# First sums of q's and k's inner products by ScalarE, and the place of three small steps, in an attention and non-local block

## The chip, the cores and the metric

The kernel runs on one core of a Trainium2 chip. The metric is the device time of one execution in microseconds; the value given for a kernel is the median of several runs. All tensors are float32.

## What is computed

The input x has 8 images of 512 channels and 32 x 32 positions. Two layers follow each other:

```
# layer 0, 8 heads of 64 channels
q, k, v = conv1x1(x, Wq, bq), conv1x1(x, Wk, bk), conv1x1(x, Wv, bv)
attn = softmax(q^T k / 8)                     # per image and head, 1024 x 1024
x = x + conv1x1(attn applied to v, Wp, bp)
# layer 1, 256 inner channels, n = 1024
g, theta, phi = conv1x1(x, ...), conv1x1(x, ...), conv1x1(x, ...)
z = conv1x1((theta phi^T / n) g, W_w, W_b) + x
out = batch norm of z over images and positions, per channel
```

A 1x1 convolution is a matrix product over the channels.

## The kernel before, in words

**Products with seven blocks.** Each convolution is a 2 x 2 block product done with seven block products instead of eight (`seven`, lines 254 to 302). The blocks of the data are differences t1 to t4 of quarters of x (`more_sums`), those of the weights are kept in DRAM with their sums. The table `SEVEN` (line 220) has one entry per block product: its name, which weight block, which data block, which PSUM slot it accumulates in, and into which quarters ("11", "12", "21", "22") of the result the slot is read when the product is there. The first read of a quarter writes it, on ScalarE or VectorE with the bias (`first`); later ones add the slot to the quarter on VectorE (`add`). A quarter has 2 x 128 channels and 512 positions; a slot has two PSUM banks, one for each 128 channels (index m), of 512 positions.

**A second level.** In q and k of images 1 to 7 three of the seven block products are themselves done with seven smaller ones (`nested`, lines 236 to 252; products 1, 6 and 2 of the outer seven, for the quarters "11", "12" and "21"), and the other four are full ones (`FOUR`, line 232). A full product has four matmuls of 128 x 128 by 512, called units here: m = 0 with both halves of the contraction, then m = 1. So a stage has 16 units. An inner product is one matmul of 128 x 128 by 256, called a step; there are 21. An inner step's result is read at once into 256 columns of q or k: added on VectorE, or written by ScalarE (line 373) where it is the first into its place. Before the change only the third of the three nested products, for "21", writes first; the quarters "11", "22" and "12" are written by ScalarE from the full products (line 380), and the inner products for "11" and "12" are added behind. The inner products alternate between two slots of PSUM; where the next one goes to the place of the last but one, it waits for the read of that.

**The order.** `STEPS` (line 233) says after which unit how many inner steps are issued; TensorE's order is fixed as written (`pe`). `fills` are small pieces of VectorE work called after certain units: the differences t3 and t4, and those for the second level of t4 (`inner_parts`); in k, the differences of the attention's output o for the projection that follows. VectorE's operations that are wrapped in `dve` keep their written order among each other; the others are placed by the framework's planner, which works with estimated durations and takes first what comes first in the program and can run. In q all adds are wrapped, in k only the fills.

**The stages of an image b**: attention (64 iterations of scores, exponential and weighted sums), then q, v, k of image b + 1, the projection of b with Wp, theta and phi, then g, the small products f and wf, and z. VectorE finds the maximum of the absolute values of each row of q and of k (lines 384 to 394, four instructions each), from which a bound on the scores is worked out (`bound_scores`, with a small matmul between the theta/phi products). In theta/phi, the functions in `between` are called after the product of that number: the maxima of k, all four, after number 1, the bound after number 4.

**The value bias.** The bias bv of the values is carried through Wp into bp once, in image 0 before the projection (`join_bias`, lines 174 to 189): GpSimd multiplies and adds Wp's rows into a tile wp_bv, eight small matmul records sum it over the channels, and VectorE adds the result to bp. wp_bv is taken from a ring of ten tiles that most temporary blocks share (`block`, line 76). The pool `w3` has three tiles with the tag "acc", for the sums of the exponentials and for g.

Of the kernel before, what the change touches and what calls it, by code (L numbers as in the profile page):

```python
# [8 lines left out]
F32 = mybir.dt.float32  # L9
I32 = mybir.dt.int32  # L10
AF = mybir.ActivationFunctionType
ALU = mybir.AluOpType
# [4 lines left out]
P = 128  # L17
# [13 lines left out]
def unshifted(ctx: ExitStack, tc: tile.TileContext, a: dict, out: bass.AP):  # L31
# [37 lines left out]
    def bank(tag, name):  # L69
        return psum.tile([P, 2, 512], F32, tag=tag, name=name)  # L70
# [5 lines left out]
    def block(name):  # L76
        return ring.tile([P, 2, 512], F32, tag="e", name=name)
# [95 lines left out]

    def join_bias(w):

        t = block("wp_bv")
        half = C // 2
        for m, quarters in enumerate(((w[:, 0], w[:, 1]), (corner["WpT"], w[:, 2]))):
            to, one = (t[:, i, m * half:(m + 1) * half] for i in range(2))
            for c in range(CC):  # L180
                nc.gpsimd.tensor_scalar(one if c else to, quarters[c // 2][:, c % 2, :], bv[:, c:c + 1], 1.0,
                                        ALU.mult, ALU.mult)
                if c:
                    nc.gpsimd.tensor_tensor(to, to, one, ALU.add)
        ps = next_bank("pbp")[:, 0, :CC]
        for oc in range(CC):
            pe(nc.tensor.matmul(ps[:, oc:oc + 1], t[:, 0, oc * P:(oc + 1) * P], ones, start=True, stop=True,
                                skip_group_check=True))
        nc.vector.tensor_tensor(bp, bp, ps, ALU.add)
# [26 lines left out]
    def quarters_of(t):  # L216
# [12 lines left out]
    FIVE = (SEVEN[0], SEVEN[1], SEVEN[2], SEVEN[3], ("s3t3", 5, "t3", 0, (("22", False), ("21", False))))  # L229


    FOUR = (SEVEN[0], ("s1t1", 3, "t1", 1, (("12", True), ("22", True))), ("s2t2", 4, "t2", 0, (("12", False),)),
            FIVE[4])
    STEPS = {2: [0] * 4 + [1] * 14, 3: [0, 0, 0, 1, 1, 2, 2, 2, 2, 2, 2, 3, 1, 1, 1, 1]}

    def nested(name, stage, w, data, tags, first, add):

        slots = [bank(tag, f"{name}_in_{tag}") for tag in tags]
        goes_to = {1: ("11", "21", False), 6: ("12", "22", False), 2: ("21", "t4", True)}
        for n, (q, di, begins) in enumerate(goes_to[i] for i in INNER[stage]):  # L240
            a, d = inner_blocks(w, stage, n), data[f"inner {di}"]
            pair = slots[::-1] if n % 2 else slots
            begun = set()
            for _, wi, di, s, reads in SEVEN:
                ps = pair[s % 2 if s < 2 else 1][:, s // 2, n % 2 * 256:(n % 2 + 1) * 256]
                pe(nc.tensor.matmul(ps, a[wi], d[di], start=s not in begun, stop=True, skip_group_check=True))  # L246
                begun.add(s)
                for to, is_first in reads:
                    c = rows(q).start + int(to[0]) - 1
                    at = cols(q).start + (int(to[1]) - 1) * 256  # L250
                    (first if is_first and begins else add)((slice(c, c + 1), slice(at, at + 256)), ps)
                yield

    def seven(name, w, data, positions_out, first, add, between=None, early=False,
              by_chunk=False, inner=None, fills=()):

        nk, half = w.shape[2], w.shape[3]
        tags = list(free)  # L260
        free[:] = [tags[3], tags[1], tags[0], tags[2]] if early else [tags[3], tags[1], tags[2], tags[0]]
        slots, begun = {}, set()
        steps, three = iter(()), inner and len(INNER[inner]) == 3
        unit, counts = 0, iter(STEPS[len(INNER[inner])] if inner else ())
        if inner:
            free[:] = [tags[1], tags[2], tags[3], tags[0]]
            steps = nested(name, inner, w, data, tags[2:], first, add)

        def read(reads, ps):
            for to, is_first in reads:  # L270
                (first if is_first else add)(to, ps)

        for n, (what, wi, di, s, reads) in enumerate(FOUR if three else FIVE if inner else EARLY if early else SEVEN):
            if s not in slots or early and what == "t4":
                slots[s] = bank(tags[s], f"{name}_{s}_{n}")
                begun -= {one for one in begun if one[0] == s}
            ps, d = slots[s], data[di]
            if positions_out:
                parts = [(ps.rearrange("p h (i f) -> p (h i) f", f=half)[:, i, :], i * half // 512,
                          lambda k, i=i: d[:, k, i * P:(i + 1) * P], lambda k: w[:, wi, k, :])  # L280
                         for i in range(512 // P)]
            else:
                parts = [(ps[:, m, :], m, lambda k, m=m: w[:, wi, k, m * P:(m + 1) * P], lambda k: d[:, k, :])
                         for m in range(half // P)]
            work = [(*part, k) for part in parts for k in range(nk)]
            if by_chunk and n == 0:
                work.sort(key=lambda one: one[4])
            for to_ps, at, lhsT, rhs, k in work:
                pe(nc.tensor.matmul(to_ps, lhsT(k), rhs(k), start=(s, at) not in begun, stop=(k == nk - 1),  # L289
                                    skip_group_check=True))  # L290
                begun.add((s, at))
                if three and unit in (3, 7, 11):
                    read(reads, ps)
                for _ in range(next(counts, 0)):
                    next(steps)
                if unit in fills:
                    fills[unit]()
                unit += 1
            if not three or n == 3:
                read(reads, ps)  # L300
            if between and n in between:
                between[n]()

# [61 lines left out]
    def heads_of(b, what, w, bias, data, pin=lambda ins: None, later=None, **how):  # L365

        t = mats.tile([P, CC, N], F32, tag=what, name=f"{what}_{b}")
        peak = small.tile([P, CC], F32, tag=f"peak_{what}", name=f"peak_{what}_{b}")

        def first(q, ps):  # L370
            if isinstance(q[0], slice):
                c = q[0].start
                nc.scalar.activation(t[:, c, q[1]], ps, AF.Identity, bias=bias[:, c:c + 1])
                return
            for m in range(2):
                c = rows(q).start + m
                if how.get("early") and q == "21":
                    nc.vector.tensor_scalar(t[:, c, cols(q)], ps[:, m, :], bias[:, c:c + 1], 1.0, ALU.add, ALU.mult)
                else:
                    nc.scalar.activation(t[:, c, cols(q)], ps[:, m, :], AF.Identity, bias=bias[:, c:c + 1])  # L380

        seven(f"p{what}_{b}", w, data, False, first, add_to(t, pin), **how)

        def peaks():
            for c in range(CC):
                ins = nc.vector.tensor_reduce(peak[:, c:c + 1], t[:, c, :], AX.X, ALU.max, apply_absolute_value=True)  # L386
                if b == 0 or later is not None:
                    dve(ins)

        if later is None:  # L390
            peaks()
        else:
            later.append(peaks)
        return t, peak

    def values(b, w, data, between=None):
# [398 lines left out]
    for b in range(B):  # L795
# [5 lines left out]
        def near_end():  # L801
            if not last:
                nxt["data"] = data_sums(quarters_of(nxt["x"]), f"x_{b + 1}", (1, 2))
                inner_sums(nxt["data"], "22")
            elif "data" not in nxt:
                nxt["data"] = data_sums(quarters_of(held["x"]), f"x1_{b - 1}_again", (1,))
            elif "t2" not in nxt["data"]:
# [9 lines left out]
        if not last:  # L817
            inner_sums(nxt["data"], "21", dve)
            later, of_t4 = [], []
            fills = {4: lambda: more_sums(nxt["data"], (3,), dve), 5: lambda: more_sums(nxt["data"], (4,), dve),  # L820
                     8: lambda: (of_t4.extend(inner_parts(nxt["data"], "t4", dve)), of_t4[0](), of_t4[1]()),
                     9: lambda: (of_t4[2](), of_t4[3]())}
            q, peak_q = heads_of(b + 1, "q", weights("WqT"), bq, nxt["data"], dve, inner="WqT",
                                 later=later, fills=fills)
            load_w(nc.sync)
# [1 line left out]
            def norm():  # L827
                nxt["products"] = normalize(denominators(next_bank(f"den_{b}")[:, 0, :]))

            v = values(b + 1, weights("WvT"), nxt["data"], {1: norm, 2: later[0], 5: lambda: nxt["products"]()})  # L830
            load_w(nc.sync)

            nxt["o"], of_21 = data_sums(quarters_of(o), f"o_{b}", ()), []
            fills = {unit: lambda i=i: more_sums(nxt["o"], (i,), dve) for unit, i in ((4, 1), (6, 2), (8, 3), (12, 4))}
            if b:
                fills[13] = lambda: (of_21.extend(inner_parts(nxt["o"], "21", dve)), of_21[0](), of_21[1]())
                fills[14] = lambda: (of_21[2](), of_21[3]())
# [30 lines left out]
        elif b > B - LATE and b != B - 2:  # L868
            z[b] = [xt[:, cc, :] for cc in range(CC)]
        tp = theta_phi(b, weights("tp"), data, {} if last else  # L870
                       {1: later_k[0], 4: lambda: bound_scores(b + 1, q, k, peak_q, peak_k)})
        load_w(nc.sync)

        def before_wf():
# [237 lines left out]
```

## Time and profile before

| | us |
|---|---|
| median of 5 runs | 2163.47 |
| lowest and highest run | 2161.86, 2164.29 |
| the profiled execution's own time | 2162.37 |
| its span, first to last instruction | 2160.5 |
| TensorE busy | 2131.9 |
| VectorE busy | 1401.3 |
| ScalarE busy | 744.8 |
| GpSimd busy | 202.0 |

The profile is of one execution. Times in it are counted from the span's start. PE is TensorE's matmul, PEld its weight load, which runs beside the matmul before; DVE is VectorE, ACT ScalarE, POOL GpSimd. An operation's line in the source is given as L and a number, and its tiles as out<-in by their names in the program: pq and pk are the PSUM slots of the full products of q and k, pq_in_s and pk_in_s those of the inner ones, ptp those of theta and phi, pbp that of the bias. One fp32 matmul of the program shows as two matmul records.

One image takes some 265 us from the start of one attention to the next; for image 2 the stages begin at 614.3 (attention), 724.3 (q of image 3), 747.5 (v), 773.1 (k), 796.3 (projection), 819.5 (theta and phi), 844.2 (g) and 866.6 (z). For image 0, k of image 1 begins at 237.8 and the projection at 264.0.

### The profile page before, as it was taken

The numbers are of one execution on the slowest core, as the hardware profiler recorded it, in microseconds if no ns is written. First come the engines' busy times: TensorE is split into PE (matmuls) and PEld (weight loads), VectorE is DVE, ScalarE is ACT, GpSimd is POOL, SyncE is SP. The second block draws the span as 40 slices with busy tenths as digits, with TensorE's granted clock in tenths as the row PEclk, the third lists the DMA queues.
The fourth block names the chain that finished last, engine by engine and source line by source line (L and its number), as shares of the span: only waits on it lengthen the run. The fifth ranks groups of instructions, "written<-read, shape, count | busy, mean of one in ns | idle before, by whom it ended". The sixth has DMA issues, their size and how long they took to land.

```text
span 2160.5 us, 30098 instructions
## 1 busy us (share of the span) xinstructions
PE 2131.9 (99%) x12510; PEld 1121.5 (52%) x12510; DVE 1401.3 (65%) x1690; ACT 744.8 (34%) x854; POOL 202.0 (9%) x256
## 2 busy tenths in 40 slices
PE   9999999999999999999999999999999999999996
PEld 4534664346733567335663366633666347643462
DVE  6467656676566675766657676576674676756736
ACT  1464103641046310463105621056212651056106
POOL 0111100110001100011000110011000110001000
PEclk9999999999999999999999999999999999999998
DMA  6333443334143331433324343233434235122758
GB/s 220 137 47 60 141 155 122 47 53 149 72 127 50 80 115 72 132 48 77 115 83 124 50 93 96 105 106 49 108 133 156 40 48 138 52 58 39 222 201 338
DMA packets 53375, 229.97 MB, mean 106 GB/s; under 512 B 9712, under 2 KB 16112, under 8 KB 45680
## 3 DMA queue, kind: packets, MB, share of 16 engines
q1 hardware_dynamic: 41552, 198.21, 27.2%
q0 software_dynamic: 10192, 28.46, 10.9%
q8 instruction: 100, 1.64, 0.3%
q10 hardware_dynamic: 1488, 1.32, 0.2%
q14 instruction: 43, 0.35, 0.0%
HBM read 140.79 MB, written 46.27 MB: 87 GB/s over the span
## 4 chain that ended last, share of the span: by engine, by line
PE 91%; DVE 5%; ACT 2%; DMA 1%; POOL 0%; issue 0%; ACTq 0%; POOLq 0%; SPq 0%
PE ps L450 20%; PE po L476 20%; PE pv L289 9%; PE pp L289 7%; PE pk L289 5%; PE pq L289 5%; PE ptp L289 5%; PE pg L289 4%; PE pq_in_s L246 3%; PE pk_in_s L246 3%; PE pf L616 3%; PE pz L289 2%; PE pp_in_s L246 2%; DVE peak_k L386 1%; PE pwf L651 1%; DVE tp L601 1%
## 5 line engine op out<-in xcount | busy, mean ns | idle before, releaser
L453 ACT ACTIVATE e<-ps 128x1024 f32<-128x1024 f32 x512 | 522.7, 1024 | 426.6 <-PE ps L450 421.1
L459 DVE TENSOR_TENSOR acc<-acc,e 128x1024 f32<-128x1024 f32 x384 | 470.0, 1224 | 144.3 <-ACT e L453 140.8
L476 PE MATMUL po<-e,v 64*64 64x512 f32 x4096 | 528.7, 589 | 0.7 <-ACT w_WgT L618 0.7
L450 PE MATMUL ps<-q,k 64*64 64x512 f32 x4096 | 529.1, 589 | 0.0
L476 PEld LDWEIGHTS po<-e,v 64*64 64x64 f32 x4096 | 156.5, 133 | 283.4 <-issue 275.7
L450 PEld LDWEIGHTS ps<-q,k 64*64 64x64 f32 x4096 | 155.6, 133 | 284.1 <-issue 275.0
L489 POOL DMA_DIRECT2D fold<-acc x189 | 147.1, 779 | 984.2 <-DMA fold<-acc 576.3
L457 DVE TENSOR_TENSOR acc<-e,e 128x1024 f32<-128x1024 f32 x64 | 78.3, 1224 | 144.0 <-ACT e L453 144.0
L639 ACT ACTIVATE g<-pg,gb 128x512 f32<-128x512 f32 x31 | 21.3, 687 | 379.6 <-PE pg L289 379.5
L289 PE MATMUL pv<-w_WvT,t_x 128*128 128x256 f32 x512 | 116.4, 381 | 0.0
L289 PE MATMUL ptp<-w_tp,t_x 128*128 128x256 f32 x512 | 115.2, 380 | 0.3
L289 PEld LDWEIGHTS pv<-w_WvT,t_x 128*128 128x128 f32 x512 | 96.6, 190 | 18.5 <-issue 5.7
L289 PEld LDWEIGHTS ptp<-w_tp,t_x 128*128 128x128 f32 x512 | 96.7, 190 | 16.0 <-DVE tp L601 3.1
L289 PE MATMUL pp<-t_o,w_WpT 128*128 128x512 f32 x208 | 100.8, 592 | 0.0
L289 PE MATMUL pq<-t_x,w_WqT 128*128 128x512 f32 x200 | 100.0, 593 | 0.8 <-DVE w_WqT L778 0.8
L289 PE MATMUL pk<-t_x,w_WkT 128*128 128x512 f32 x200 | 100.0, 592 | 0.0
L417 POOL TENSOR_SCALAR q<-q,gates 128x1024 f32<-128x1024 f32 x32 | 35.1, 1109 | 676.3 <-DVE gates L415 582.4
L405 ACT COPY v<-pv 128x1024 f32<-128x1024 f32 x32 | 32.4, 1012 | 173.2 <-PE pv L289 173.2
L289 PE MATMUL ptp<-w_tp,x 128*128 128x256 f32 x384 | 87.4, 381 | 0.0
L289 PE MATMUL pv<-w_WvT,x 128*128 128x256 f32 x384 | 86.8, 379 | 0.0
L289 PEld LDWEIGHTS ptp<-w_tp,x 128*128 128x128 f32 x384 | 72.4, 190 | 13.0 <-issue 3.6
L289 PEld LDWEIGHTS pv<-w_WvT,x 128*128 128x128 f32 x384 | 73.0, 190 | 10.3 <-issue 0.2
(179 smaller groups left out, 2255.3 us busy)
## 6 DMA issues: line engine op xcount, KB each, us to landing
fold<-acc POOLq DMA_DIRECT2D x189, 128.0 KB, 3.1
w_WqT<-kept_WqT SPq DMA_DIRECT2D x7, 2368.0 KB, 8.8
w_WkT<-kept_WkT SPq DMA_DIRECT2D x7, 2368.0 KB, 9.0
r<-den_d SPq DMA_DIRECT2D x32, 512.0 KB, 7.5
x<-in_x_dram SPq DMA_DIRECT2D x31, 512.0 KB, 5.9
w_WpT<-kept_WpT SPq DMA_DIRECT2D x6, 2176.0 KB, 8.5
w_WvT<-kept_WvT SPq DMA_DIRECT2D x7, 1792.0 KB, 7.1
w_tp<-kept_tp SPq DMA_DIRECT2D x7, 1792.0 KB, 7.2
```

Source lines behind the costliest of these rows:

```text
L246: pe(nc.tensor.matmul(ps, a[wi], d[di], start=s not in begun, stop=True, skip_group_check=True))
L289: pe(nc.tensor.matmul(to_ps, lhsT(k), rhs(k), start=(s, at) not in begun, stop=(k == nk - 1), skip_group_check=True))
L386: ins = nc.vector.tensor_reduce(peak[:, c:c + 1], t[:, c, :], AX.X, ALU.max, apply_absolute_value=True)
L405: seven(f"pv_{b}", w, data, True, lambda q, ps: nc.scalar.copy(at(q), as_v(ps)), lambda q, ps: dve(nc.vector.tensor_tensor(at(q), at(q), a ...
L417: nc.gpsimd.tensor_scalar(q[:, p, :], q[:, p, :], gate[:, p:p + 1], 1.0, ALU.mult, ALU.mult)
L450: pe(nc.tensor.matmul(ps[c * P // 2:(c + 1) * P // 2, j, :], k[r, p, keys], q[r, p, h * 512:(h + 1) * 512], start=True, stop=True, skip_gr ...
L453: nc.scalar.activation(e, ps, AF.Exp, scale=SCALE)
L457: nc.vector.tensor_tensor(accs[u], es[u, 0], e, ALU.add)
L459: ins = nc.vector.tensor_tensor(accs[u], accs[u], e, ALU.add)
L476: pe(nc.tensor.matmul(ps[j * D:(j + 1) * D, r, :], v[keys, m, (2 * p + j) * D:(2 * p + j + 1) * D], e[keys, j, :], start=(m == 0), stop=(m ...
L489: nc.gpsimd.dma_start(to, part_of, accum_op=ALU.add)
L616: pe(nc.tensor.matmul(ps[:, c, :], tp[:, i, c * P:(c + 1) * P], tp[:, i, CI:], start=(i == 0), stop=(i == NB - 1)))
```

## The change

- In q and k with three nested products, the first read of every place by an inner product is a write with the bias on ScalarE, for all three nested products. The full products of "11" and "12" are added behind by VectorE; the product "11" in slot 0 by halves (m = 0 after unit 6 and ahead of its steps, m = 1 behind them), the product into "12" in slot 0 by halves too (after units 9 and 11, ahead of the steps). "22" is still written first from slot 1 by ScalarE, now behind unit 9, and slot 1 is added to "12" by VectorE behind unit 11. The last product is added to "22" and "21" at the end, as before.
- `STEPS` for three nested products is arranged anew, with at most two steps behind a unit.
- The fills of q move from units 4, 5, 8, 9 to 3, 4, 5, 7; the first two of k from 4 and 6 to 3 and 5.
- The four maxima of k are called in pairs after theta/phi's products 1 and 2. Those of q are called together where they were.
- wp_bv is taken from the pool `w3` with the tag "acc", not from the ring.
- The four inner differences of "22" at the end of an attention keep their written order on VectorE.

```diff
     def join_bias(w):
-        t = block("wp_bv")
+        t = w3.tile([P, 2, 512], F32, tag="acc", name="wp_bv")
...
-    FOUR = (SEVEN[0], ("s1t1", 3, "t1", 1, (("12", True), ("22", True))), ("s2t2", 4, "t2", 0, (("12", False),)),
-            FIVE[4])
-    STEPS = {2: [0] * 4 + [1] * 14, 3: [0, 0, 0, 1, 1, 2, 2, 2, 2, 2, 2, 3, 1, 1, 1, 1]}
+    FOUR = tuple((*one[:4], ()) for one in (SEVEN[0], SEVEN[1], SEVEN[2], FIVE[4]))
+    AHEAD = {6: ((0, 0, "11", False),), 9: ((0, 0, "12", False),), 11: ((0, 1, "12", False),)}
+    BEHIND = {6: ((0, 1, "11", False),), 9: ((1, None, "22", True),), 11: ((1, None, "12", False),),
+              15: ((0, None, "22", False), (0, None, "21", False))}
+    STEPS = {2: [0] * 4 + [1] * 14, 3: [0, 0, 0, 1, 2, 2, 2, 2, 1, 2, 2, 2, 2, 1, 1, 1]}
...
-                    (first if is_first and begins else add)((slice(c, c + 1), slice(at, at + 256)), ps)
+                    (first if is_first and (begins or three) else add)((slice(c, c + 1), slice(at, at + 256)), ps)
...
+        def read_parts(parts):
+            for s, m, to, is_first in parts if three else ():
+                if m is None:
+                    read(((to, is_first),), slots[s])
+                else:
+                    c = rows(to).start + m
+                    read((((slice(c, c + 1), cols(to)), is_first),), slots[s][:, m, :])
...
-                if three and unit in (3, 7, 11):
-                    read(reads, ps)
+                read_parts(AHEAD.get(unit, ()))
                 for _ in range(next(counts, 0)):
                     next(steps)
+                read_parts(BEHIND.get(unit, ()))
                 if unit in fills:
                     fills[unit]()
                 unit += 1
-            if not three or n == 3:
-                read(reads, ps)
+            read(reads, ps)
...
-                inner_sums(nxt["data"], "22")
+                inner_sums(nxt["data"], "22", dve)
...
-            fills = {4: lambda: more_sums(nxt["data"], (3,), dve), 5: lambda: more_sums(nxt["data"], (4,), dve),
-                     8: lambda: (of_t4.extend(inner_parts(nxt["data"], "t4", dve)), of_t4[0](), of_t4[1]()),
-                     9: lambda: (of_t4[2](), of_t4[3]())}
+            fills = {3: lambda: more_sums(nxt["data"], (3,), dve), 4: lambda: more_sums(nxt["data"], (4,), dve),
+                     5: lambda: (of_t4.extend(inner_parts(nxt["data"], "t4", dve)), of_t4[0](), of_t4[1]()),
+                     7: lambda: (of_t4[2](), of_t4[3]())}
...
-            fills = {unit: lambda i=i: more_sums(nxt["o"], (i,), dve) for unit, i in ((4, 1), (6, 2), (8, 3), (12, 4))}
+            fills = {unit: lambda i=i: more_sums(nxt["o"], (i,), dve) for unit, i in ((3, 1), (5, 2), (8, 3), (12, 4))}
...
-                       {1: later_k[0], 4: lambda: bound_scores(b + 1, q, k, peak_q, peak_k)})
+                       {1: lambda: [one() for one in later_k[:2]], 2: lambda: [one() for one in later_k[2:]],
+                        4: lambda: bound_scores(b + 1, q, k, peak_q, peak_k)})
```

More of the change, by code (lines that the diff above doesn't have):

```diff
@@ L229, in unshifted @@
     FIVE = (SEVEN[0], SEVEN[1], SEVEN[2], SEVEN[3], ("s3t3", 5, "t3", 0, (("22", False), ("21", False))))
-    FOUR = (SEVEN[0], ("s1t1", 3, "t1", 1, (("12", True), ("22", True))), ("s2t2", 4, "t2", 0, (("12", False),)),
-            FIVE[4])
-    STEPS = {2: [0] * 4 + [1] * 14, 3: [0, 0, 0, 1, 1, 2, 2, 2, 2, 2, 2, 3, 1, 1, 1, 1]}
+    FOUR = tuple((*one[:4], ()) for one in (SEVEN[0], SEVEN[1], SEVEN[2], FIVE[4]))
[3 more added lines that the diff above has]
+    STEPS = {2: [0] * 4 + [1] * 14, 3: [0, 0, 0, 1, 2, 2, 2, 2, 1, 2, 2, 2, 2, 1, 1, 1]}
     def nested(name, stage, w, data, tags, first, add):
-        slots = [bank(tag, f"{name}_in_{tag}") for tag in tags]
+        slots, three = [bank(tag, f"{name}_in_{tag}") for tag in tags], len(INNER[stage]) == 3
         goes_to = {1: ("11", "21", False), 6: ("12", "22", False), 2: ("21", "t4", True)}
@@ L382, in heads_of, with peak_of @@
         seven(f"p{what}_{b}", w, data, False, first, add_to(t, pin), **how)
[L384 to L393, printed above, removed]
+        def peak_of(c):
+            ins = nc.vector.tensor_reduce(peak[:, c:c + 1], t[:, c, :], AX.X, ALU.max, apply_absolute_value=True)
+            if b == 0 or later is not None:
+                dve(ins)
+        for c in range(CC):
+            if later is None:
+                peak_of(c)
+            else:
+                later.append(lambda c=c: peak_of(c))
         return t, peak
@@ L828, in norm @@
                 nxt["products"] = normalize(denominators(next_bank(f"den_{b}")[:, 0, :]))
-            v = values(b + 1, weights("WvT"), nxt["data"], {1: norm, 2: later[0], 5: lambda: nxt["products"]()})
+            v = values(b + 1, weights("WvT"), nxt["data"], {1: norm, 2: lambda: [one() for one in later], 5: lambda: nxt["products"]()})
             load_w(nc.sync)
             nxt["o"], of_21 = data_sums(quarters_of(o), f"o_{b}", ()), []
-            fills = {unit: lambda i=i: more_sums(nxt["o"], (i,), dve) for unit, i in ((4, 1), (6, 2), (8, 3), (12, 4))}
+            fills = {unit: lambda i=i: more_sums(nxt["o"], (i,), dve) for unit, i in ((3, 1), (5, 2), (8, 3), (12, 4))}
             if b:
```

## The prediction

> **What bounds the kernel now.** I read the page's first part, then the chain of work that ended last, then the waits, and then TensorE's timeline inside one image.
>
> ```profile
> PE 2131.9 (99%) x12510; PEld 1121.5 (52%) x12510; DVE 1401.3 (65%) x1690; ACT 744.8 (34%) x854; POOL 202.0 (9%) x256
> ...
> PE 91%; DVE 5%; ACT 2%; DMA 1%; POOL 0%; issue 0%; ACTq 0%; POOLq 0%; SPq 0%
> ```
>
> TensorE (PE) is busy for 2131.9 of 2160.5 us, and the change removes no matmul. So it can win only stretches in which TensorE stands still or runs slowly, and it loses by making new ones. Work given from VectorE (DVE, 65%) to ScalarE (ACT, 34%) is worth nothing by itself. The stretches inside an image are short; the waits name them:
>
> ```profile
> POOL wp_bv L181 <- PE pk L289: 45.6, 1, 45.6
> ...
> PEld pq_in_s L246 <- ACT q L373: 3.7, 7, 0.5
> PEld pk_in_s L246 <- ACT k L373: 3.7, 7, 0.5
> PEld ptp L289 <- DVE tp L601: 3.1, 7, 0.4
> ...
> PEld pbp L187 <- POOL wp_bv L184: 2.2, 2, 1.4
> ```
>
> The columns are: who waited, for whom, us in total, times, longest. Seven times each (once per image) a weight load waits for ScalarE in q and in k, and for VectorE in theta/phi; once the bias waits for GpSimd (POOL). How much of such a wait TensorE itself feels, its timeline shows (start, duration; a group of two records is one fp32 matmul):
>
> ```profile
> 739.83 1.02 PE L289 MATMUL pq<-t_x,w_WqT 128*128 128x512 f32 x2
> 740.69 0.59 PE L246 MATMUL pq_in_s<-t_x,w_WqT 128*128 128x256 f32 x2
> 741.12 1.43 PE L246 MATMUL pq_in_s<-i_t_x,w_WqT 128*128 128x256 f32 x4
> 742.38 1.02 PE L289 MATMUL pq<-t_x,w_WqT 128*128 128x512 f32 x2
> ```
>
> From start to start a full matmul (a unit) takes 0.86 us and an inner one (a step) 0.43. The two steps from 741.12 should end at 741.98; the next unit starts at 742.38. That is a **stall of 0.40 to 0.41**: three steps stand in a row, and the third writes the bank whose first product ScalarE reads only from 741.32:
>
> ```profile
> 741.32 0.91 ACT L373 ACTIVATE q<-pq_in_s,bq 128x256 f32<-128x256 f32 x2 [4.90 <-PE pq_in_s L246]
> ```
>
> The product ends at 741.12, the read begins 0.20 later and takes 0.47, and TensorE goes on some 0.16 after it: a bank is blocked for 0.83 us from the end of its product, and one step covers 0.43. I counted the rest of q and of k against 0.86 and 0.43: apart from 0.1 to 0.2 at q's start nothing else is lost. The group of 1.43 stands in all fourteen stages.
>
> [...] The stall of 0.40 is a write held back by a read of the very same columns, so this trace does not tell bank from address; I take the bank, the stricter of the two. [...] The trace shows one such window in the body, right after image 0's k:
>
> ```profile
> 261.91:265.33 3.42, 2.38 (x11) 1.65 (x12) 2.13 (x4) 0.00 (x0) 1.51 (x3) 1.00 0.76 228
> 265.33:268.74 3.41, 3.41 (x5) 1.33 (x4) 0.69 (x1) 0.00 (x0) 0.00 (x0) 0.50 0.02 5
> ```
>
> The column before the last two is the granted clock: 0.50 for 3.41 us, following a window in which TensorE mostly waited for the bias. [...] Here, beside GpSimd's bias work, a difference t_o took 1.51 us instead of 1.22 and a GpSimd sum up to 1.71 instead of 0.72[...].
>
> **Part by part.** *Inner products in q and k.* Removed: the stall, for the new table of steps has at most two in a row: 14 x 0.41 = 5.7 us. Moved: of 21 inner reads per stage ScalarE now does 12 (4 before), VectorE 9 (17); ScalarE writes 2 full halves (0.6 each) where it wrote 6; VectorE gets 4 half adds (0.61 apart) for "11" and "12", and keeps three whole ones. VectorE: 8 x 0.34 less, 4 x 0.61 more, about 0.3 less; ScalarE: 8 x 0.45 more, 4 x 0.6 less, 1.2 more in a stage of 23 us with 70% idle. Both are beside TensorE.
>
> Does a new wait come? I placed the new order with 0.86 and 0.43 from the stage's start. Between a bank's product and the next into it there is now at least a unit and a step, 1.29 us, against 0.83 needed: **0.46 to spare**, also where two products come together, as ScalarE's second read then ends 0.44 after the first. VectorE is free of the preceding attention 4.4 us into q (728.71 less 724.30). Then t3 and t4 (1.14 each) end at 6.7, the adds of steps 3 and 4 at 7.9 (ready at 7.1; needed at 8.4), the two differences at 8.6, and the first half of "11" at 9.2. Unit 8 overwrites that half at 10.75: **1.4 to spare**. The second half waits for step 6 on ScalarE (9.7) and ends at 10.4; behind it on VectorE are the last two differences, wanted at 16.8. Around unit 9 the half add of "12" and two inner adds end at 14.5, and step 13 wants the bank at 15.05: 0.4 to spare. In k the products of the normalisation end at 2.8, and t2_o stands ahead of "11": that half is read by 9.6, 1.0 to spare. The last two whole adds begin at the stage's end as before. ScalarE's pair for "22" may be queued late, as written, or early, when slot 1 is complete: 1.2 us in front of inner reads that have 0.46 to spare, of which much then has arrived anyway; from 0 to 0.4 per stage, and I take 0.
>
> *Earlier differences* (fills), pinned order in the end of attention: 0 us; the trace already has that order, and their ring slots are released. The cover is VectorE's idle time; without it the 1.0 above shrinks.
>
> *Maxima of k in pairs.* Now four of 1.13 stand between two theta/phi sums:
>
> ```profile
> 829.69 3.62 PE L289 MATMUL ptp<-w_tp,x 128*128 128x256 f32 x16
> 833.36 3.72 PE L289 MATMUL ptp<-w_tp,t_x 128*128 128x256 f32 x16
> ```
>
> and on VectorE beside it:
>
> ```profile
> 827.58 4.59 DVE L386 TENSOR_REDUCE peak_k<-k 128x1 f32<-128x1024 f32 x4
> 832.09 1.21 DVE L601 TENSOR_TENSOR tp<-ptp,tpb 128x1024 f32<-128x1024 f32 x1
> ```
>
> Sixteen records take 3.455 elsewhere; here 3.67 pass: 0.21 lost, as slot 0 is read only at 832.1 to 833.2. After two maxima (to 829.85) that read runs 829.9 to 831.1, two us early; the other pair ends at 833.4 and the bound's matmul wants it at 836.9. Saved 7 x 0.21 = **1.5 us**; next late is nothing for 2 us.
>
> *Value bias.* wp_bv waited for a ring slot (45.6 above) until 254.6; its inputs were asked for from 237.9, landing in 3.0 to 6.4 us, so from about 244 it can run in another pool whose slot's last user is long done. Its 14 instructions took 8.9 us: done by about 254, and k's matmuls end at 261.1. TensorE then stood to 264.03, 2.91 us; the eight bias records themselves need some 1.04 (0.52 for four loads), so **1.9 us** goes. With it I let the half-clock window go: 3.41 x 0.5 = **1.7 us**; bounds 0 and 1.7, and the first is a rival. Against it, GpSimd now works beside k's weight sums on VectorE; eight or so such operations longer by up to 0.3 each, with 0.4 to spare: 0 to 0.6, I take 0.3.
>
> **Sum.** 5.7 + 1.5 + 1.9 + 1.7 - 0.3 = 10.5 us. The profiled execution took 2162.37 (span 2160.5) and would take 2151.9; the median of the runs is 1.1 higher, 2163.47, and gives **2153.0**. For this case alone 2150.5 to 2155.5: the unknown 0 to 0.6 and 0 to 1.7, and runs that lie 1.2 around their median.
>
> **Rivals.** (1) *The half-speed window stays*[...]: 1.7 less, 2154.7. [...] Against: idle time there falls from 2.9 to about 1. (2) *A wait takes the place of the one removed*: ScalarE's "22" pair or VectorE's half adds hold an inner bank 0.4 longer than its 0.46, in each stage. Then the 5.7 goes back: 2158.7, gain 4.8. For it: spares of 0.4 are thin; against: no other engine is near full there. (3) *Slower*: the first half of "11", until now read by ScalarE at unit 3, is behind VectorE's queue. If VectorE comes to it two long differences (2 x 1.14 = 2.3) later than I placed it, unit 8 stalls by 2.3 less 1.2 (mean of 1.4 and 1.0), 1.1 in each of 14 stages, and the later adds push on the next stage: 15.4 lost, with the rest 4.9 net, 2168.4. It costs from 1.0 to 1.4 us of lateness on, and outweighs all gains from about 2.0. For it: k's adds are not pinned, so the planner may put the pinned differences first; against: the trace of before keeps the written order in both stages.
>
> **How the numbers follow.** Forecast 0.56; rival 1 0.08; rival 2 0.23; rival 3 0.13. About 0.2%, 4.3 us, is what a measurement of this kernel can tell from no change. Rival 2 lies close to that edge: I put 0.10 of it faster, 0.13 within. Faster 0.56 + 0.08 + 0.10 = 0.74, same 0.13, slower 0.13. The range runs from the forecast's low end, 2150.5, past rival 2 with 2.3 on top, 2161.0, and leaves out mainly rival 3.
>
> **What would show it.** Right: no group of four inner records over 1.03 us in q and k; the two waits on ScalarE at L373 gone or without a gap on TensorE; q and k 0.4 shorter; 3.46 between the fourth and fifth theta/phi product; wp_bv's first instruction near 244 and no granted 0.50 near 265. Wrong: a wait of full matmuls (pq, pk at their line) for VectorE at the start of the third product, or of inner ones for ScalarE, seven times each, or wp_bv still starting after 254.

## The result and the profile after

The changed kernel takes 2166.45 us (median of 27 runs, 2165.44 to 2167.21). The kernel before, run beside it, takes 2162.0 (47 runs, 2160.06 to 2164.29). The ratio is 1.0021, with a 95% interval from 1.0016 to 1.0026: slower by 4.5 us, with the interval clear of no change. The forecast was 10.5 us faster. The profiled execution took 2166.16 us with a span of 2164.5, against 2162.37 and 2160.5 before.

The page's busy times and its chain of work that ended last:

```profile
PE 2133.9 (99%) x12510; PEld 1121.5 (52%) x12510; DVE 1395.4 (64%) x1634; ACT 761.3 (35%) x910; POOL 205.4 (9%) x256
...
PE 95%; ACT 2%; DVE 1%; DMA 1%; issue 0%; SPq 0%; DVEq 0%; ACTq 0%
```

TensorE has the same 12510 instructions, and the work did move: VectorE is 5.9 us lighter and ScalarE 16.5 heavier. TensorE's share of the chain even rose, from 91 to 95%, while the time grew. So neither of these views says where the time went. The waits do (who waited, for whom, us in total, times, longest):

```profile
POOL wp_bv L181 <- DMA w_WpT<-in_WpT_dram: 32.1, 1, 32.1
...
PEld pk_in_s L249 <- DVE k L323: 16.2, 28, 1.6
...
PEld pq_in_s L249 <- DVE q L323: 9.8, 28, 0.7
...
PEld pk_in_s L249 <- ACT k L383: 6.7, 28, 0.2
PEld pq_in_s L249 <- ACT q L383: 6.4, 27, 0.2
```

The seven long waits of a weight load for ScalarE (0.5 each) are gone from q and from k; short ones of at most 0.2 have come. But in k an inner product now waits up to 1.6 us for VectorE. TensorE's timeline in k of image 3 shows it (start, duration):

```profile
779.06 0.60 PE L249 MATMUL pk_in_s<-x,w_WkT 128*128 128x256 f32 x2
779.49 0.59 PE L249 MATMUL pk_in_s<-i_x,w_WkT 128*128 128x256 f32 x2
779.92 1.02 PE L300 MATMUL pk<-t_x,w_WkT 128*128 128x512 f32 x2
781.70 0.70 PE L249 MATMUL pk_in_s<-x,w_WkT 128*128 128x256 f32 x2 [0.76 <-DVE k L323]
782.24 0.60 PE L249 MATMUL pk_in_s<-i_x,w_WkT 128*128 128x256 f32 x2
...
785.25 0.60 PE L249 MATMUL pk_in_s<-i_x,w_WkT 128*128 128x256 f32 x2
785.83 1.13 PE L300 MATMUL pk<-t_x,w_WkT 128*128 128x512 f32 x2
786.79 0.60 PE L249 MATMUL pk_in_s<-x,w_WkT 128*128 128x256 f32 x2
```

I count units and steps from 0, as the tables in the code do. These lines are steps 5 and 6, unit 7, then steps 7 and 8. Unit 7 starts at 779.92, so step 7 is due at 780.78; it starts at 781.70, **0.92 late**, and step 8 comes 0.54 after it instead of 0.43, another 0.11. Further down unit 10 is due at 785.68 and starts at 785.83, and the step behind it comes after 0.96 instead of 0.86: 0.15 and 0.10. Unit 12 loses the same 0.25. VectorE's timeline beside it:

```profile
778.04 0.78 DVE L323 TENSOR_TENSOR k<-k,pk_in_s 128x256 f32<-128x256 f32 x2 [2.46 <-PE pk_in_s L249]
778.74 1.22 DVE L201 TENSOR_TENSOR t_o<-o,t_o 128x1024 f32<-128x1024 f32 x1
779.87 1.45 DVE L323 TENSOR_TENSOR k<-k,pk 128x512 f32<-128x512 f32 x2
781.24 0.41 DVE L323 TENSOR_TENSOR k<-k,pk_in_s 128x256 f32<-128x256 f32 x1
781.57 1.22 DVE L201 TENSOR_TENSOR t_o<-o 128x1024 f32<-128x1024 f32 x1
```

Step 5's product is there at 779.49, but its add is the line at 781.24, behind t2_o (the difference t2 of o) and behind both halves of "11". It ends at 781.65, and step 7 starts at 781.70. Step 5 lies in bank 1 of its slot and step 7 goes to bank 0 of the same slot: they share the slot, not the bank. What stood in bank 0 before was step 3's product, and its add was done by 778.82 (the first line holds the adds of steps 3 and 4).

The two other parts of the change did what they were to do. TensorE in theta and phi of image 2:

```profile
828.79 3.62 PE L300 MATMUL ptp<-w_tp,x 128*128 128x256 f32 x16
832.25 3.62 PE L300 MATMUL ptp<-w_tp,t_x 128*128 128x256 f32 x16
```

and VectorE beside it:

```profile
826.68 2.34 DVE L395 TENSOR_REDUCE peak_k<-k 128x1 f32<-128x1024 f32 x2
829.00 1.22 DVE L611 TENSOR_TENSOR tp<-ptp,tpb 128x1024 f32<-128x1024 f32 x1
830.14 2.33 DVE L395 TENSOR_REDUCE peak_k<-k 128x1 f32<-128x1024 f32 x2
```

From start to start 3.46 pass, where 3.67 did, and the read of slot 0 stands between two pairs of maxima. Image 0's bias:

```profile
261.51 0.59 PE L249 MATMUL pk_in_s<-i_t_x,w_WkT 128*128 128x256 f32 x2
261.94 0.95 PE L187 MATMUL pbp<-ones,wp_bv 128*128 128x1 f32 x8
262.75 3.68 PE L300 MATMUL pp<-o,w_WpT 128*128 128x512 f32 x8
```

The eight records follow k at once, with no gap, and the projection follows them. The stretch behind them, by busy time of each engine and then the granted clock (the third column from the end):

```profile
264.91:268.32 3.41, 3.41 (x9) 1.52 (x8) 2.54 (x4) 0.00 (x0) 0.00 (x0) 1.00 0.25 78
```

Full speed, 1.00, where the kernel before had 0.50.

Stage lengths, from one stage's first matmul to the next one's, show where the time is (us; theta and phi is one stage):

| stage | before | after | difference, with its count |
|---|---|---|---|
| q of images 1 to 7 | 23.31 | 23.53, the last 23.88 | +1.9 (6 x 0.22 and 0.57) |
| k of image 1 | 24.62 | 24.44 | -0.2 |
| k of images 2 to 7 | 23.20 | 24.33 | +6.8 (6 x 1.13) |
| theta and phi of images 0 to 6 (image 6: 0.09 more in both) | 24.71 | 24.40 | -2.2 (7 x 0.31) |
| bias and projection of image 0 | 1.73 + 25.81 | 0.81 + 24.12 | -2.6 |
| last projection | 24.29 | 24.86 | +0.6 |
| q of image 0 | 25.73 | 25.33 | -0.4 |

The sum is +3.9, the spans differ by 4.0. The last two rows move by some tenths from kernel to kernel where nothing of theirs is changed (q of image 0 takes between 25.10 and 25.97 in the profiles below, the last projection between 24.10 and 24.86), and I don't read them.

### The profile page after: what moved, and what is told of

Its sections match the earlier page's. It is cut to its first block, busy times and chain, and to the rows that moved or that the text cites. A ratio compares the mean times of both kernels' runs of the same rounds, so it can differ in the third digit from the quotient of the medians.

```text
span 2164.5 us, 30088 instructions
## 1 busy us (share of the span) xinstructions
PE 2133.9 (99%) x12510; PEld 1121.5 (52%) x12510; DVE 1395.4 (64%) x1634; ACT 761.3 (35%) x910; POOL 205.4 (9%) x256
## 4 chain that ended last, share of the span: by engine, by line
PE 95%; ACT 2%; DVE 1%; DMA 1%; issue 0%; SPq 0%; DVEq 0%; ACTq 0%
PE ps L460 20%; PE po L486 20%; PE pv L300 9%; PE ptp L300 9%; PE pp L300 7%; PE pq L300 5%; PE pk L300 5%; PE pg L300 4%; PE pq_in_s L249 3%; PE pk_in_s L249 3%; PE pf L626 3%; PE pz L300 2%; PE pp_in_s L249 2%; PE pwf L661 1%; ACT z L777 1%; PE den L432 0%
## 5 line engine op out<-in xcount | busy, mean ns | idle before, releaser
L383 ACT ACTIVATE k<-pk_in_s,bk 128x256 f32<-128x256 f32 x84 | 38.9, 473 | 116.2 <-PE pk_in_s L249 116.2
```

## The experiments

**The theory.** In this program a matmul that writes one bank of a PSUM slot of two waits for the reads of the other bank too. So step 7 hangs on VectorE's add of step 5, unit 10 on the first half add of "12", unit 12 on the second. In k, where the adds aren't pinned (kept in their written order), the planner put step 5's add last behind t2_o and "11"; that was brought about by calling t2_o behind unit 5 instead of unit 6. **The rivals:** the wait is by bank, and VectorE is simply later than placed in this stretch, because there is more to do in it; or the loss isn't in q and k's inner products at all but comes with the bias or the maxima.

**The two small parts alone, and the inner products alone.** The first is the kernel before with these lines, and with the maxima made single functions that can be called apart:

```diff
-        t = block("wp_bv")
+        t = w3.tile([P, 2, 512], F32, tag="acc", name="wp_bv")
...
-                       {1: later_k[0], 4: lambda: bound_scores(b + 1, q, k, peak_q, peak_k)})
+                       {1: lambda: [one() for one in later_k[:2]], 2: lambda: [one() for one in later_k[2:]],
+                        4: lambda: bound_scores(b + 1, q, k, peak_q, peak_k)})
```

> The kernel before with only the bias tile in the other pool and k's maxima in pairs. Both theories: the stage sums of the two traces give theta/phi 7 x 0.31 = 2.2 us less and image 0's projection and bias 2.6 us less, so 4.8 us less than before (ratio 0.9978). If the half-speed window that the trace of before shows at 265 us is not usual in its runs, 1.7 of that is missing: 3.1 us less.

The second is the kernel after with the same two undone:

```diff
-        t = w3.tile([P, 2, 512], F32, tag="acc", name="wp_bv")
+        t = block("wp_bv")
...
-                       {1: lambda: [one() for one in later_k[:2]], 2: lambda: [one() for one in later_k[2:]],
+                       {1: lambda: [one() for one in later_k],
```

> The changed kernel with the bias tile back in the ring and the four maxima together again; only the inner products, their steps and the fills are new. Both theories: q 7 x 0.2 and k 7 x 1.13 more, 9.4 us or somewhat less above before (ratio 1.004); if the sum of the parts does not hold, it is nearer to the changed kernel's 4.5 us.

Measured: the small parts alone 2156.61 (11 runs; before, beside it, 2161.64 in 31), ratio 0.9979, interval 0.997 to 0.9988. The inner products alone 2172.11 (5 runs), ratio 1.0048, interval 1.0034 to 1.0062. Added up, -5.0 and +10.5 are +5.5, near the +4.5 of the whole. All of the loss is in the inner products' part; the third idea is out. Of all kernels here the first is the fastest.

**The maxima alone**, to part the two small ones: the kernel before with only the second of those edits.

> The kernel before with k's maxima in pairs and nothing else. 7 x 0.31 = 2.2 us less than before (ratio 0.9990); the bias tile's part is then what is missing to the kernel with both, 2.6 to 2.8, of which 1.7 is the half-speed window.

Measured 2159.16 (13 runs; before 2161.3 in 25), ratio 0.9991, interval 0.9982 to 0.9999. Theta and phi take 24.40 instead of 24.71, seven times: 2.2 us. The bias stage is as before, 1.73. In this profile, with a mean granted clock of 0.996, the half-speed stretch is missing all the same: image 0's projection takes 24.12, though the stops at the bias are still there.

**k's adds in the written order.** All of k's adds are pinned, as q's are. In k of images 2 to 7 only one pair of neighbours changes places on VectorE: step 5's add comes ahead of the second half of "11". (In image 1 a sum of Wp's blocks, which isn't pinned, moves ahead of that add too.)

```diff
-            k, peak_k = heads_of(b + 1, "k", weights("WkT"), bk, nxt["data"], later=later_k, inner="WkT",
+            k, peak_k = heads_of(b + 1, "k", weights("WkT"), bk, nxt["data"], dve, later=later_k, inner="WkT",
```

> The changed kernel with k's adds in their written order, as q's are: in each k the inner add of step 5 stands ahead of the second half of '11' instead of behind it, and nothing else moves. Theory (a write waits for the read of the other bank of its slot, so step 7 waits for step 5's add behind VectorE's queue): the add comes 0.6 to 0.7 earlier, k loses 0.2 instead of 0.9 there, 7 x 0.7 = 4.9 us less than the changed kernel, about level with before. Rival (VectorE has too much to do in the first half of k, in whatever order): no change against the changed kernel, 4.5 us above before.

Measured 2162.79 (13 runs; before 2161.64), ratio 1.0006, interval 0.9997 to 1.0014; k of images 3 to 7 takes 23.77 instead of 24.33, that of image 2 24.12, that of image 1 24.61. TensorE in k of image 3:

```profile
780.20 1.02 PE L300 MATMUL pk<-t_x,w_WkT 128*128 128x512 f32 x2
781.41 0.70 PE L249 MATMUL pk_in_s<-x,w_WkT 128*128 128x256 f32 x2 [0.19 <-DVE k L323]
```

and VectorE:

```profile
779.02 1.22 DVE L201 TENSOR_TENSOR t_o<-o,t_o 128x1024 f32<-128x1024 f32 x1
780.15 0.68 DVE L323 TENSOR_TENSOR k<-k,pk 128x512 f32<-128x512 f32 x1
780.94 0.42 DVE L323 TENSOR_TENSOR k<-k,pk_in_s 128x256 f32<-128x256 f32 x1
781.27 0.68 DVE L323 TENSOR_TENSOR k<-k,pk 128x512 f32<-128x512 f32 x1
```

Step 5's add now ends at 781.36, and step 7 starts at 781.41 (due at 781.06), although the second half of "11" is still to be done. VectorE's work in the stretch is the same; only the place of this one add moved, and step 7 moved with it. So step 7 waits for this add. A mere load of the stretch, the first rival, would have given no gain. The gain falls short of the 4.9 expected: k's seven stages are 2.8 us shorter. Step 7 is still 0.35 late, for 0.2 expected, and in image 1, where the sum of Wp's blocks (1.06 us) went ahead of the add, it is 1.20 late; unit 10 of image 2 is 0.35 later than in the other images, which I did not follow.

**t2_o later.** The same with t2_o behind unit 7, and then the changed kernel with nothing but t2_o back behind unit 6, k's adds left to the planner:

```diff
-            fills = {unit: lambda i=i: more_sums(nxt["o"], (i,), dve) for unit, i in ((3, 1), (5, 2), (8, 3), (12, 4))}
+            fills = {unit: lambda i=i: more_sums(nxt["o"], (i,), dve) for unit, i in ((3, 1), (7, 2), (8, 3), (12, 4))}
```

> As the kernel with k's written order, and the difference t2_o called after unit 7 instead of unit 5, so that it stands behind step 5's add. Theory: the wait of step 7 is gone entirely, 7 x 0.92 = 6.4 us less than the changed kernel, 2 us below before; what stays in k are two waits of 0.14 at the third product. Rival: about half of that, since the 1.14 us of t2_o are only moved within the same crowded stretch.

```diff
-            fills = {unit: lambda i=i: more_sums(nxt["o"], (i,), dve) for unit, i in ((3, 1), (5, 2), (8, 3), (12, 4))}
+            fills = {unit: lambda i=i: more_sums(nxt["o"], (i,), dve) for unit, i in ((3, 1), (6, 2), (8, 3), (12, 4))}
```

> The changed kernel with one number put back: in k the difference t2_o is called after unit 6, as before the change, instead of unit 5; k's adds stay unpinned. In the program VectorE's order in k is then half of '11', step 5's add, the other half, t2_o. Theory (order on VectorE decides, not its load): as with the written order and t2_o later, 6.4 us less than the changed kernel, 2.6 us below before, k at 23.3. Rival (the load of the stretch): t2_o moved by one unit changes little, under 2 us.

Measured: 2159.0 (13 runs; before 2161.64), ratio 0.9991, interval 0.9982 to 0.9999; and 2159.12 (13 runs; before 2161.3), ratio 0.999, interval 0.9982 to 0.9999. Steady k (images 3 to 7) takes 23.30 and 23.31. VectorE with t2_o behind unit 6:

```profile
777.22 0.68 DVE L323 TENSOR_TENSOR k<-k,pk 128x512 f32<-128x512 f32 x1
778.17 0.42 DVE L323 TENSOR_TENSOR k<-k,pk_in_s 128x256 f32<-128x256 f32 x1 [0.27 <-PE pk_in_s L249]
779.11 0.69 DVE L323 TENSOR_TENSOR k<-k,pk 128x512 f32<-128x512 f32 x1 [0.52 <-ACT k L383]
779.72 1.22 DVE L201 TENSOR_TENSOR t_o<-o,t_o 128x1024 f32<-128x1024 f32 x1
```

and TensorE, unit 7 and then step 7:

```profile
778.40 1.02 PE L300 MATMUL pk<-t_x,w_WkT 128*128 128x512 f32 x2
779.26 0.59 PE L249 MATMUL pk_in_s<-x,w_WkT 128*128 128x256 f32 x2
```

Step 7 starts when it is due, 0.86 after unit 7. One digit changes, and without a pin the planner takes the first half, step 5's add, the second half, and t2_o last; VectorE even stands idle ahead of two of them. Step 7's wait is gone from k (24.33 less 23.31 is 1.02, the 0.92 and 0.11 above). So one difference called one unit too early, with what it made of the planner's order, cost 7 x 1.03 = 7.2 us at step 7. Some 0.5 of it comes back at unit 10 in k of images 1 and 2, so that k's seven stages are 6.7 us shorter (6.4 were expected); the two ratios differ by 0.0031, also 6.7.

**Step 5 in the other slot**, to tell slot from bank. In the kernel with k's adds pinned and t2_o behind unit 7, step 5 of the first nested product is given the other slot's bank 1:

```diff
-                ps = pair[s % 2 if s < 2 else 1][:, s // 2, n % 2 * 256:(n % 2 + 1) * 256]
+                ps = pair[s % 2 if s < 2 else int(n > 0)][:, s // 2, n % 2 * 256:(n % 2 + 1) * 256]
```

> The kernel with the written order and t2_o later, with step 5 of the first nested product put into the second bank of the other slot. Theory (a write waits for reads of either bank of its slot): step 6, which writes the first bank of that slot directly behind step 5, has to wait for step 5's add, 0.2 + 0.4 + 0.06 us and a late weight load of 0.1 in place of nothing, some 0.75 in each of 14 stages, 10 us more than that kernel. Rival (the wait is by bank): step 6 waits for step 4 alone as before, no change.

Measured 2173.78 (5 runs; before 2161.3), ratio 1.0058, interval 1.0045 to 1.0072. TensorE in k of image 3:

```profile
783.39 0.59 PE L249 MATMUL pk_in_s<-x,w_WkT 128*128 128x256 f32 x2
784.50 0.70 PE L249 MATMUL pk_in_s<-i_x,w_WkT 128*128 128x256 f32 x2 [0.51 <-DVE k L323]
785.03 1.02 PE L300 MATMUL pk<-t_x,w_WkT 128*128 128x512 f32 x2
```

and VectorE:

```profile
782.37 0.78 DVE L323 TENSOR_TENSOR k<-k,pk_in_s 128x256 f32<-128x256 f32 x2 [3.21 <-PE pk_in_s L249]
...
784.02 0.42 DVE L323 TENSOR_TENSOR k<-k,pk_in_s 128x256 f32<-128x256 f32 x1 [0.27 <-PE pk_in_s L249]
```

Step 5 starts at 783.39 and step 6 is due at 783.82. They write different banks of what is now one slot, and step 6 starts at 784.50, just behind the end of step 5's add at 784.44. By bank nothing would hold it: step 6 writes over step 4, and the adds of steps 3 and 4, the first of these lines, end at 783.15. The wait is **by slot**, and the wait by bank falls. A slot is one tile of 128 x 2 x 512 in the kernel, its two banks together (`bank`, line 69 in the kernel before); no run here tells the tile from the pair of banks, or what in the program or below it sets the wait. Steady k takes 24.09 instead of 23.30, 0.79 more. In q the same edit costs 1.29 (24.82 instead of 23.53): there two differences and the half of "11" stand ahead of the add on VectorE, so that it comes later. Expected were 0.75 in each of the 14 stages, 10 us; by the ratios it is 14.5, q being the difference. The same edit moves step 5 in the projections, whose length stays 23.21.

**q's differences later.** With t2_o behind unit 6, the fills of the inner differences of t4 go from units 5 and 7 to 7 and 8, out of the way of step 5's add in q:

```diff
-                     5: lambda: (of_t4.extend(inner_parts(nxt["data"], "t4", dve)), of_t4[0](), of_t4[1]()),
-                     7: lambda: (of_t4[2](), of_t4[3]())}
+                     7: lambda: (of_t4.extend(inner_parts(nxt["data"], "t4", dve)), of_t4[0](), of_t4[1]()),
+                     8: lambda: (of_t4[2](), of_t4[3]())}
```

> As t2o at unit 6, and in q the first two differences of t4's second level are called after unit 7 and the other two after unit 8, so that nothing stands ahead of the half of '11' and step 5's add on VectorE. Theory: the last 0.11 at step 7 of q goes, q from 23.53 to 23.42, 0.8 us in all, 2158.3; two waits of 0.25 each at units 10 and 12 stay in q and in k, so that q and k remain above the 23.31 and 23.20 of before. Rival (the order ahead of step 5 has nothing to do with q's loss): q stays at 23.53.

Measured 2158.75 (20 runs; before 2160.63 in 23), ratio 0.9988, interval 0.9982 to 0.9995; q takes 23.41 instead of 23.53 (23.76 in image 7, not followed), k 23.30. The ratios alone, 0.9990 and 0.9988, don't tell this kernel from the one with t2_o behind unit 6; the stage lengths do. What is left in q, on TensorE:

```profile
734.52 1.12 PE L300 MATMUL pq<-t_x,w_WqT 128*128 128x512 f32 x2
735.48 0.59 PE L249 MATMUL pq_in_s<-x,w_WqT 128*128 128x256 f32 x2
```

and on VectorE:

```profile
733.77 0.69 DVE L323 TENSOR_TENSOR q<-q,pq 128x512 f32<-128x512 f32 x1 [1.28 <-PE pq L300]
```

The half add of "12" (m = 0) begins as soon as its product is there and ends at 734.46; unit 10, which writes m = 1 of the same slot, starts at 734.52, 0.15 late, with 0.10 behind it. VectorE was idle for 1.28 ahead of this add, so no shorter queue would help: these two waits, 0.25 each, belong to the order of units and half adds itself. Making the slot's two banks two tiles might free them; that wasn't tried.

## Why the prediction was wrong

**The order of events, counted out.** I compared TensorE's starts in a steady stage with 0.86 and 0.43 for each unit and step. What is over them:

| us lost in a steady stage | before | after | t2_o at unit 6 | and q's differences later |
|---|---|---|---|---|
| q: at its start | 0.10 | 0.10 | 0.10 | 0.10 |
| q: three steps in a row | 0.40 | 0 | 0 | 0 |
| q: step 7 | 0 | 0.10 | 0.10 | 0 |
| q: units 10 and 12 | 0 | 0.50 | 0.50 | 0.50 |
| k: three steps in a row | 0.40 | 0 | 0 | 0 |
| k: step 7 | 0 | 1.03 | 0 | 0 |
| k: units 10 and 12 | 0 | 0.50 | 0.50 | 0.50 |

*Inner products, forecast -5.7.* **This is the term that fell**: q and k together are 8.5 us longer, and some 9.8 without the 1.3 that k of image 1 won by the bias; the earlier differences (next but one) have their part in this. The stall of 0.40 did go, as the table has it. The step that failed is "Between a bank's product and the next into it there is now at least a unit and a step, 1.29 us, against 0.83 needed: **0.46 to spare**", with its ground, "I take the bank, the stricter of the two". The bank isn't the stricter one in this program: a wait by slot adds pairs of instructions that the bank doesn't know, and I never listed them. Step 7 on step 5's add is one, units 10 and 12 on half adds of "12" are two more. The 1.29 is there for step 7 too, from the end of step 5 at 779.49 to 780.78. But 0.83 was ScalarE's price with nothing queued; step 5 is read by VectorE, which had 2.5 us of other work ahead of it (778.74 to 781.24), and so 2.21 were needed, until 781.70. The 0.83 itself was read from a group of records. One weight load of the kernel before parts it:

```profile
741.85 0.30 PEld L246 LDWEIGHTS pq_in_s<-i_t_x,w_WqT 128*128 128x128 f32 x2 [0.53 <-ACT q L373]
```

The third step goes on at 741.85, 0.73 after the product's end; the other 0.10 came at the start behind it, as in the last section. That a write waits by bank was my estimate, from a stall that shows a write and a read of the same columns alone; with step 5 in the other slot, step 6 started 0.68 late, 0.06 behind the end of the read of the other bank, and that decides for the slot here.

*What would have been left.* With t2_o at unit 6 and q's differences later, where step 7 no longer waits, each stage still loses 0.50 for the 0.40 it won. So even at its best here this part gains nothing: q 23.41 and k 23.30 against 23.31 and 23.20 before. That is 1.4 us lost where 5.7 were to be won, about half of the 15 us between forecast and result.

*The earlier differences, forecast "0 us".* Wrong by the other half: 6.7 us, by t2_o in k, which went from unit 6 to 5, and 0.8 in q (7 x 0.12), by the differences of t4. "The cover is VectorE's idle time; without it the 1.0 above shrinks" saw that it hangs on VectorE's queue, but followed the wrong instruction in it: the half of "11" that unit 8 overwrites, and not the add of step 5, which the planner put behind both halves. Unit 8 itself didn't wait.

*Maxima in pairs, forecast -1.5.* Right in mechanism and place (3.46 from start to start); theta and phi are 0.31 shorter rather than 0.21, so 2.2. The other 0.10 lies behind the late group: the bound's matmul comes 3.55 after it in the kernel before (833.36 to 836.91) and 3.45 in the changed one (832.25 to 835.70). That is the size of a late wait's cost in the last section.

*Value bias, forecast -1.9, -1.7 and +0.3.* Right in the stops; in the window in part by luck. Three of wp_bv's instructions, on the quarter of Wp that lies ready, now run from 200.7 on; the others wait for the rest of Wp until 240.7 (forecast: about 244). In the kernel with the two small parts alone the stops at the bias, 1.18 ahead of its first record and 0.92 more behind it, 2.10 in all, are gone and k of image 1 has new stops of 0.8 in front of matmuls that wait for VectorE, where VectorE's sums run beside GpSimd's (two sums of Wp's blocks took 1.00 and 1.12 there, for 0.68 and 0.69 in the kernel before); the forecast allowed 0.3 for that. Net, k of image 1, the bias and the projection are 3.0 shorter there, against 3.3; 1.69 of it is the projection, without the half-speed window. That window was in the profile from which the forecast was made, but it isn't in all executions (last section), and it is missing with the bias untouched in the profile of the maxima alone. That it goes with the stop at the bias was my estimate; what brings it was not shown. What stood ahead of it was not "mostly" waiting either: TensorE was busy for 2.38 of those 3.42 us.

*The rivals.* The third had the kind of mechanism that happened: VectorE's queue in k, with the pinned difference taken first. It had the wrong place and the wrong reach, unit 8 in all 14 stages and 15.4 us; it was step 7, in seven stages and for 7.2, with 14 x 0.50 more at units 10 and 12. The ground against it, that "the trace of before keeps the written order in both stages", was no ground: the planner decided anew, since the program was new. The second, a wait in place of the stall, came true in size at units 10 and 12, but through VectorE's half adds and the slot, not through an inner bank. The first didn't happen: all runs on record of the changed kernel have the same mean clock, 0.996.

## What to carry to other kernels

Before an order of matmuls is changed, list for each one the reads of the whole slot that it writes to, and not only of the columns it overwrites: here step 6 started 0.68 late, behind a read of the other bank. Then follow each of these reads through its engine's queue. A small piece of work that is pinned and moved a place earlier isn't free where others around it are left to a planner (t2_o cost 7.2 us at step 7): look for what is queued behind it, and who waits for that. In this program, halving the read of "12" didn't let unit 10 go: it writes m = 1, and started at 734.52, 0.06 behind the end of the half add of m = 0.

## What the runs showed beside

- **A late wait cost 0.10 more than itself.** Where a matmul group of q and k waited for a read (0.15 at unit 10, 0.35 or 0.92 at step 7), the next start came 0.10 to 0.11 later than the usual distance (0.96 for 0.86, 0.54 for 0.43). By the table of waits the waiting instruction is mostly the weight load (in k of the changed kernel 28 waits of it for VectorE, 16.2 us, and 7 of the matmul itself, 5.3); that it then isn't hidden beside a matmul is my reading of the 0.10, not shown by itself.
- **By the mean clock, the half-speed window came only in some executions of the kernel before.** Of the 31 runs beside the first experiments 14 had a mean granted clock of 0.996 and a median of 2160.11, and 17 one of 0.994 or 0.995 and 2161.88. The 1.8 between them is about half of a window of 3.41. (The profile of the kernel before, with the window, has 0.995; that of the maxima alone, without it, 0.996.) In the changed kernel and in the one with the two small parts alone all runs had 0.996. Over all kernels here the lower clock stands in 48 of 97 runs with the bias in its old place, and in 2 of 104 with it moved. So moving the bias took away a chance of the lower clock as well as a stop; if the lower clock is that window in each of these runs (my reading, from the profiles alone), that is worth about 1 us on average, not 1.7.
